# Planning a four-layer graph kernel with repeated forward and backward passes

## The chip, the cores and the metric

The kernel runs on one core of a Trainium2 chip. A core has TensorE (PE: matrix products and transposes, into PSUM), VectorE (DVE), ScalarE (ACT), GpSimd (POOL) and SyncE (SP, which here only issues DMAs). Each engine takes its instructions in the order in which the program lists them and waits for the operands of the one at its head. The metric is the device time of the core in microseconds.

## The reference, cut to what matters

128 graphs of 64 nodes each carry 256 features per node; `adj` holds 0 or 1 for every pair of nodes. Four graph layers follow each other, each on the normalised input and with a residual:

```python
# layer 0: attention with 4 heads, W [256, 256]
h = jnp.maximum(_layernorm(x, axis=-1), 0.0)
x = x + _L0_gnn_ref(h, adj, L0_gnn_W, L0_gnn_a_src, L0_gnn_a_dst)
# layer 1: attention with one head
h = jnp.maximum(_layernorm(x, axis=-1), 0.0)
x = x + _L1_gnn_ref(h, adj, L1_gnn_W, L1_gnn_a)
# layer 2: relational convolution; only relation 1 ("loop") can occur with these edges
h = jnp.maximum(_layernorm(x, axis=-1), 0.0)
x = x + _L2_gnn_ref(h, nodemask, adj, ...)
# layer 3: gated graph convolution, three steps
h = jnp.maximum(_layernorm(x, axis=-1), 0.0)
x = x + _L3_gnn_ref(h, adj, L3_gnn_weight, L3_gnn_w_ih, L3_gnn_w_hh, L3_gnn_b_ih, L3_gnn_b_hh)
```

An attention layer takes `Wh = h @ W`, scores `leaky_relu(e_src[i] + e_dst[j])`, a softmax over the neighbours j of i, and adds `elu(alpha @ Wh)`. The loop relation adds `relu(A^T @ ((h W + b) * sigmoid(h W Wg + bg)))`. A step of layer 3 is a GRU cell:

```python
for i in range(3):
    m = jnp.einsum('bnd,de->bne', h, weight[i])
    aggr = jnp.einsum('bst,bsd->btd', A, m)
    h = _gru_cell(aggr, h, w_ih, w_hh, b_ih, b_hh)   # r, z: sigmoid; n: tanh
```

## The kernel before, in words

**Tiles.** The 8192 rows (graph and node) form 16 groups of four 128-row tiles: 512 rows, eight graphs. All four layers of a group run in SBUF; rows are read once and written once. All is float32. A product streams up to 512 columns through a 128x128 weight; the profile records two passes for each product and one for a transpose.

**Layers 0 to 2** (jobs `(g, p0, layer)`). Each begins with a layer norm and a turned copy `hT`. For groups 0 and 1, which run in halves of two tiles, the turn is made by TensorE transposes (`layernorm_T`); from group 2 on by a 32x32 DVE transpose and 16 DMAs on SP (`layernorm_T_by_dma`, `hT<-hn` in the profile). `attention` needs the source score of every node along the free dimension. From group 2 on it sends it through DRAM: `tp<-fs`, `fT<-tp`, DMA `row<-fT`, two DMAs `t<-row`, all on SP; then DVE makes `t` from it, and `aggregate_graphs` multiplies it with the values in 64x64 quadrants, recorded by `beside` (`mm`, `mn` at L609). `loop_relation` is like it with the edges themselves.

**Layer 3.** Job `("before", g)` normalises and aggregates once more. Job `("recur", g)` runs three GRU steps over transposed states, in two chunks of 128 features (`Chunk`). Products add up in PSUM banks `ry`, `rm`, `rz`, `nh`, `ni`; one bank, `ry`, is filled and emptied in turn by ACT or DVE. The 128-row halves of a state are combined by a seven-product scheme, whose sums of states (`hS`, `aS`) GpSimd makes. DVE ends a step with `d<-z,d` and `hT<-d,t`; `along` aggregates the new state for the next step (`tp`, `tq` at L609, copied to `aT` by ACT). GpSimd makes `d<-hT,t`.

**Weights.** Job `"weights"` transposes the loop relation's weights (`wn`, `gn`) and the GRU's (`hhn`, `ihn`), and multiplies the latter with `weight[i]` (`wrn`). They are loaded by SP in the job "more loads", after the rows of groups 0 and 1.

**What sets the order.** No instruction is issued where it is written. An engine's method (`Engine.__getattr__`; the emitting line is L388, so that nearly every row of the profile says L388) only notes an operation: its engine, its cost in ns from a table, what it reads and writes, its job. `Plan.emit` then places all of them. Each has a due time, worked out from hand-set starts and ends of the jobs (`start, period = 87.96, 83.9`, with offsets for each layer) and from the length of the chain behind the operation; where a job has no end, from its successors. The planner repeatedly takes, among all operations whose predecessors are placed and whose buffers are free, the one that can start first, and of several such the one due first. Engines are modelled with 170.8 ns between them, DMAs as one wire, and DVE and GpSimd as sharing a port. The order in which operations are placed is the program's, and Tile puts the waits between them. Buffers come from pools with a few copies (`Pool.place`, `put`); PSUM's from `Banks`, where, until a bank of layer 3 has been used, the other layers may borrow the first four of those.

Where the model leaves TensorE idle for over 320 ns before 115 us, and layer 3 has not begun, it adds a product of ones that nobody reads for every 220 ns (`nc.spare`, `ni<-warm` at L1322).

Of the kernel before, what the change touches and what calls it, by code (L numbers as in the profile page):

```python
# [45 lines left out]
ENGINES = {"tensor": "PE", "vector": "DVE", "scalar": "Activation", "gpsimd": "Pool", "sync": "SP"}  # L46
# [81 lines left out]
class Base:  # L128


    def __init__(self, pool, shape, dtype, name, tag, bufs):
        self.pool, self.make, self.tag, self.bufs = pool, (shape, dtype, name), tag, bufs
        self.real, self.left, self.end, self.writes, self.reads = None, 0, 0.0, [], []
        self.whole = False


class Pool:
# [5 lines left out]
    def __init__(self, real=None, bufs=1, ordered=()):  # L143
        self.real, self.bufs, self.ordered = real, bufs, ordered
        self.live, self.asked = {}, {}

    def tile(self, shape, dtype, name, tag=None, bufs=None):
        tag = tag or name
        base = Base(self, shape, dtype, name, tag, bufs or self.bufs)
        if tag in self.ordered:  # L150
            self.asked.setdefault(tag, []).append(base)
        return View(base, shape, (), [(0, n) for n in shape], list(range(len(shape))))

    def place(self, base, taken):

        if self.real is None:
            return None
        if base.tag in self.ordered and self.asked[base.tag][0] is not base:
            return None
        live = [b for b in self.live.get(base.tag, ()) if b.left]  # L160
        return base.tag if len(live) + taken.count(base.tag) < base.bufs else None
# [12 lines left out]
    def put(self, base, tag):  # L174
        shape, dtype, name = base.make
        base.real = self.real.tile(shape, dtype, name=name, tag=tag, bufs=base.bufs)
        if base.tag in self.ordered:
            self.asked[base.tag].pop(0)
        live = self.live.setdefault(tag, [])
        if len(live) >= self.room(tag, base):  # L180
            live.remove(min((b for b in live if not b.left), key=lambda b: b.end))
        live.append(base)
# [17 lines left out]
class Job:  # L200
# [3 lines left out]
    def __init__(self, start, end, after):  # L204
        self.start, self.end, self.after, self.left, self.length = start, end, after, 0, 0.0
        self.spread = 1.86


class Plan:
# [21 lines left out]
    def kept(self, pool, shape, dtype, name):  # L231

        view = Pool().tile(shape, dtype, name)
        view.base.real = pool.tile(shape, dtype, name=name)
        return view
# [4 lines left out]
    def note(self, engine, call, cost, writes, reads, after=(), port=0.0, dma=False):  # L240
        op = Op(engine, call, cost, port, dma, self.job, len(self.ops))
        self.ops.append(op)
        self.job.left += 1
# [20 lines left out]
        for b in op.bases:  # L264
            b.left += 1
        return op

    def emit(self):

        self.on = False  # L270
# [11 lines left out]
        for op in self.ops:  # L282
            op.waits = len(op.after)
            for other in op.after:
                other.then.append(op)
# [3 lines left out]
        for op in reversed(self.ops):  # L289
            if op.job.end is None:  # L290
                op.due = 1e9
                for t in op.then:
                    late = 0.0 if t.engine == op.engine else self.LATENCY
                    op.due = min(op.due, t.due - op.job.spread * (op.cost + late))
            else:
                op.due = (op.job.end - (op.job.end - op.job.start) * op.tail / op.job.length) * 1e3
        free = dict.fromkeys([*ENGINES.values(), "-"], 0.0)
        early = {"DVE": 83.0, "Activation": 95.0, "Pool": 43.0}
        ready = {e: [] for e in free}
        wire = 2500.0  # L300
        held = {"DVE": 0.0, "Pool": 0.0}

        def enter(op):
            t = 0.0
            for other, data in op.after.items():
                late = other.end + self.LATENCY
                if other.engine == op.engine and not (other.dma and data):
                    late = other.start if op.engine in ("PE", "SP") or not data else other.end + 35.0
                t = max(t, late)
            op.ready = t  # L310
            ready[op.engine].append(op)

# [3 lines left out]
        left = len(self.ops)  # L316
        while left:
            best = None
            for e, ops in ready.items():
                found = None  # L320
                for op in ops:
                    t = max(free[e], op.ready)
                    if best is not None and t > best[0] or found is not None and t > found[0] and t > free[e]:
                        continue
                    if any(j.left for j in op.job.after):
                        continue
                    places = {}
                    for b in op.needs:
                        if b.real is None:
                            taken = [tag for x, tag in places.items() if x.pool is b.pool]  # L330
                            tag = b.pool.place(b, taken)
                            if tag is None:
                                break
                            places[b] = tag
                            t = max(t, b.pool.released(tag, b, taken.count(tag)))
                    else:
                        key = (t, op.due)
                        if found is None or key < found[:2]:
                            found = (*key, op, places)
                if found is not None and (best is None or found[:2] < best[:2]):  # L340
                    best = found
            assert best is not None, "nothing can be emitted"
            t, _, op, places = best
            e = op.engine
            ready[e].remove(op)
            if e == "PE" and self.spare and t < 115.0 * 1e3:
                for _ in range(int((t - free[e] - 100.0) / 220.0)):
                    self.spare()
            for b, tag in places.items():
                b.pool.put(b, tag)  # L350
            op.call()
            op.start = t
            if op.dma:
                free[e] = t + 665.0
                wire = max(wire, t + 1350.0) + op.cost
                op.end = wire + 400.0
            else:
# [6 lines left out]
                free[e] = t + took - min(early.get(e, 0.0), op.cost / 2)  # L364
# [4 lines left out]
            left -= 1  # L369
            for other in op.then:  # L370
                other.waits -= 1
                if not other.waits:
                    enter(other)
        self.ops = []
        return max(free.values())
# [69 lines left out]
def kernel(  # L445
# [506 lines left out]
    with ExitStack() as s1:  # L952
# [4 lines left out]
        class Banks(Pool):  # L957
# [4 lines left out]
            early = psum = True  # L962
# [8 lines left out]

            def place(self, base, taken):
                if base.tag in self.own:
                    return super().place(base, taken)
                for tag in ("mt", *self.own[: 4 if 115.0 else 5]) if self.early else ("mt",):
# [5 lines left out]
            def put(self, base, tag):  # L981
                base.bufs = self.room(tag, base)
                if base.tag in self.own:
                    self.early = False
                super().put(base, tag)
# [332 lines left out]
        if 115.0:  # L1318
# [3 lines left out]
            nc.spare = lambda: psum.early and nc.nc.tensor.matmul(pause, warm, warm, start=True, stop=True)  # L1322
# [217 lines left out]
```

## Time and profile before

| what | value |
|---|---|
| runs, device time | 1431.6 us median of 3 (1430.19 to 1432.47) |
| profiled execution: span | 1428.7 us |
| median of the runs less that span | 2.9 us |
| PE, share of span | 98% |
| DVE, ACT, POOL | 72%, 57%, 42% |
| DMA | 67.89 MB, mean 48 GB/s |
| warm products (`ni<-warm`) | 242 records, 32.2 us |
| `hT<-hn` DMAs | 896 of 32 KB |

Engine times are busy time; where one engine waits for another and nothing is late for it, the idle time costs nothing. The span is that of one profiled execution, whose durations the rows give; the runs' time includes something before and after it. A float32 product has two records. "Idle before" names what ended the wait of the first instruction behind it.

One group takes about 84 us in the middle of the kernel. While layer 3 of group g runs, TensorE also does layers 0 to 2 of later groups, in the gaps of the recurrence. At the start only groups 0 and 1 and the weights are there; at the end only the last group's recurrence. So three stretches differ: before 115 us, after 1345 us, and between them.

### The profile page before, as it was taken

The numbers are of one execution on the slowest core, as the hardware profiler recorded it, in microseconds if no ns is written. First come the engines' busy times: TensorE is split into PE (matmuls) and PEld (weight loads), VectorE is DVE, ScalarE is ACT, GpSimd is POOL, SyncE is SP. The second block draws the span as 40 slices with busy tenths as digits, with TensorE's granted clock in tenths as the row PEclk, the third lists the DMA queues.
The fourth block names the chain that finished last, engine by engine and source line by source line (L and its number), as shares of the span: only waits on it lengthen the run. The fifth ranks groups of instructions, "written<-read, shape, count | busy, mean of one in ns | idle before, by whom it ended". The sixth has DMA issues, their size and how long they took to land.

```text
span 1428.7 us, 27951 instructions
## 1 busy us (share of the span) xinstructions
PE 1403.0 (98%) x9703; PEld 964.6 (68%) x9703; DVE 1027.9 (72%) x2553; ACT 808.1 (57%) x2045; POOL 600.5 (42%) x744
## 2 busy tenths in 40 slices
PE   9999999999999999999999999999999999999997
PEld 8666666767667666766766676676667666666664
DVE  6658677785958869685886968688686958665544
ACT  3665556565555655655565565556556555554543
POOL 1454344445424444543444354344435434352422
PEclk9999999999999999999999999999999999999998
DMA  8010222222223122222312222231212122111000
GB/s 219 22 20 20 42 60 37 59 44 41 61 49 71 32 63 42 45 60 49 72 31 63 42 46 60 48 72 30 59 28 44 45 45 54 26 22 28 16 15 18
DMA packets 299420, 67.89 MB, mean 48 GB/s; under 512 B 274696, under 2 KB 297480, under 8 KB 299272
## 3 DMA queue, kind: packets, MB, share of 16 engines
q1 hardware_dynamic: 298712, 65.50, 22.0%
q8 instruction: 80, 1.31, 0.4%
q14 instruction: 68, 0.56, 0.1%
q10 hardware_dynamic: 560, 0.52, 0.1%
HBM read 28.06 MB, written 8.53 MB: 26 GB/s over the span
## 4 chain that ended last, share of the span: by engine, by line
PE 88%; DVE 5%; ACT 2%; DMA 2%; SPq 1%; issue 1%; POOL 1%; DVEq 0%; ACTq 0%; POOLq 0%
PE ry L388 22%; PE mm L388 16%; PE rz L388 11%; PE ni L388 10%; PE nh L388 10%; PE rm L388 5%; PE tp L388 4%; PE mm L609 3%; PE tp L609 3%; PE ni L1322 2%; DVE t L388 1%; DMA t<-row 1%; SPq L388 1%; DVE d L388 1%; DVE hT L388 1%
## 5 line engine op out<-in xcount | busy, mean ns | idle before, releaser
L388 POOL TENSOR_TENSOR d<-hT,t 128x256 f32<-128x256 f32 x192 | 143.2, 754 | 485.1 <-ACT t L388 479.8
L388 PE MATMUL ni<-aT,wc 128*128 128x512 f32 x384 | 194.6, 595 | 0.0
L388 PE MATMUL nh<-hT,whh 128*128 128x512 f32 x384 | 193.6, 597 | 0.0
L388 DVE SCALAR_TENSOR_TENSOR t<-r,t 128x256 f32<-128x256 f32 x192 | 110.9, 582 | 66.2 <-ACT r L388 43.4
L388 ACT ACTIVATE z<-z,brz 128x256 f32<-128x256 f32 x192 | 96.8, 504 | 90.4 <-DVE z L388 90.2
L388 ACT COPY z<-ry 128x256 f32<-128x256 f32 x192 | 70.9, 369 | 130.3 <-PE ry L388 86.8
L388 POOL TENSOR_TENSOR hS<-hT 128x256 f32<-128x256 f32 x96 | 79.4, 833 | 121.6 <-PE ry L388 84.5
L388 PE MATMUL ry<-hS,wsum 128*128 128x256 f32 x384 | 117.3, 387 | 2.6 <-ACT z L388 2.6
L388 PE MATMUL rz<-hS,whh 128*128 128x256 f32 x384 | 117.5, 388 | 2.2 <-DVE z L388 2.1
L388 ACT ACTIVATE hn<-xg,var,rstd 128x256 f32<-128x256 f32 x200 | 107.4, 594 | 13.1 <-DVE var L388 12.7
L388 PE MATMUL mm<-wl,hT 128*128 128x512 f32 x248 | 114.7, 597 | 0.1
L388 PE MATMUL ry<-aS,wsum 128*128 128x256 f32 x384 | 114.5, 380 | 0.0
L388 PE MATMUL rz<-aS,wc 128*128 128x256 f32 x384 | 114.4, 380 | 0.0
L388 DVE SCALAR_TENSOR_TENSOR hT<-d,t 128x256 f32<-128x256 f32 x192 | 110.8, 593 | 4.3 <-ACT fd L388 0.5
L388 DVE SCALAR_TENSOR_TENSOR d<-z,d 128x256 f32<-128x256 f32 x192 | 101.1, 537 | 17.2 <-ACT z L388 10.5
L388 ACT ACTIVATE t<-t,bi 128x256 f32<-128x256 f32 x192 | 93.9, 502 | 29.2 <-DVE t L388 28.8
L388 DVE TENSOR_TENSOR t<-t,gd 128x512 f32<-128x512 f32 (+2 forms) x48 | 29.8, 645 | 107.8 <-DMA t<-row 95.3
L388 DVE TENSOR_TENSOR z<-rz,z 128x256 f32<-128x256 f32 x192 | 80.0, 417 | 34.3 <-ACT z L388 17.4
L388 PEld LDWEIGHTS ry<-hS,wsum 128*128 128x128 f32 x384 | 69.4, 190 | 44.5 <-issue 25.3
L388 POOL TENSOR_TENSOR aS<-aT,aS 128x256 f32<-128x256 f32 x96 | 74.0, 772 | 57.8 <-ACT aT L388 57.7
L388 DVE BATCH_NORM_STATS2 st<-xg 128x6 f32<-128x256 f32 x256 | 93.3, 408 | 2.7 <-DMA xg<-in_x_dram 2.7
L388 POOL TENSOR_TENSOR hS<-hT,hS 128x256 f32<-128x256 f32 x96 | 74.7, 778 | 43.9 <-DVE hT L388 43.0
(205 smaller groups left out, 3268.9 us busy)
## 6 DMA issues: line engine op xcount, KB each, us to landing
hT<-hn SPq DMA_DIRECT2D x896, 32.0 KB
xg<-in_x_dram SPq DMA_DIRECT2D x15, 512.0 KB
out_dram<-hnat SPq DMA_DIRECT2D x15, 512.0 KB
t<-row SPq DMA_DIRECT2D x28, 256.0 KB
at<-in_adj_dram SPq DMA_DIRECT2D x64, 32.0 KB
eg<-in_adj_dram SPq DMA_DIRECT2D x64, 32.0 KB
ag<-in_adj_dram SPq DMA_DIRECT2D x16, 128.0 KB
t<-row SPq DMA_DIRECT2D x28, 64.0 KB
```

Of the source, the lines that this page charges most:

```text
L388: return do(*[real(a) for a in args], **{k: real(v) for k, v in kwargs.items()})
L609: nc.nc.tensor.matmul(*[real(x) for x in product], start=True, stop=True)
L1322: nc.spare = lambda: psum.early and nc.nc.tensor.matmul(pause, warm, warm, start=True, stop=True)
```

## The change

The costs, jobs and instructions stay, and so do the hand-set times, for the first pass. The planner is split and repeated. `link` works out the dependencies and the first due times once. `forward` makes a whole order; an engine may now choose, among operations that can start within a leeway of the earliest (100 ns; SP 300), the one due first, and so stand idle until it is ready. `backward` goes through that order's program from its end and gives every operation the latest time at which it could start, counting dependencies, the engine it runs on and the reuse of buffers that this pass had (`replaced`); those are the due times of the next pass. After 40 passes the order with the smallest modelled end is emitted. The pools place buffers in the model and make the tiles when the chosen order is emitted. Warm products are added in that order's idle stretches by the same rule.

```diff
+    PASSES = 40
+    LEEWAY = {"PE": 100.0, "DVE": 100.0, "Activation": 100.0, "Pool": 100.0, "SP": 300.0, "-": 0.0}
+    OVERLAP = {"DVE": 83.0, "Activation": 95.0, "Pool": 43.0}
+    ISSUE = 665.0
+    def link(self):
...
+            op.busy = self.ISSUE if op.dma else op.cost - min(self.OVERLAP.get(op.engine, 0.0), op.cost / 2)
...
+    def forward(self):
+        for b in self.bases:
+            b.left, b.end, b.spot = len(b.ops), 0.0, None
...
             for e, ops in ready.items():
-                found = None
+                leeway, first, found = self.LEEWAY[e], 1e18, []
                 for op in ops:
-                    t = max(free[e], op.ready)
-                    if best is not None and t > best[0] or found is not None and t > found[0] and t > free[e]:
+                    t = op.ready if op.ready > free[e] else free[e]
+                    if t > first + leeway or best is not None and t > best[0] + leeway:
                         continue
...
+                    places, t = spots(op, t)
+                    if places is not None:
+                        first = min(first, t)
+                        found.append((t, op, places))
+                found = [(t, op.due, op, places) for t, op, places in found if t <= first + leeway]
+                if found:
+                    found = min(found, key=lambda f: (f[1], f[0]))
+                    if best is None or found[:2] < best[:2]:
+                        best = found
...
-            if e == "PE" and self.spare and t < 115.0 * 1e3:
-                for _ in range(int((t - free[e] - 100.0) / 220.0)):
-                    self.spare()
...
+            for b, tag in op.places:
+                old = b.pool.put(b, tag)
+                if old is not None:
+                    self.replaced.append((old, op))
...
+    def backward(self, end):
+        before, left = {}, {}
+        for op in self.ops:
+            op.late, op.waits = 1e18, len(op.then)
+            before[op] = []
+        for old, op in self.replaced:
+            for other in old.ops:
+                if other is not op:
+                    before[op].append(other)
+                    other.waits += 1
+        free = dict.fromkeys([*ENGINES.values(), "-"], end)
+        ready = {e: [op for op in self.ops if op.engine == e and not op.waits] for e in free}
+        for op in self.ops:
+            op.took = min(op.end - op.start, 4500.0) if op.dma else op.end - op.start
...
+        for _ in self.ops:
+            best = None
+            for e, ops in ready.items():
+                for op in ops:
+                    key = (min(free[e], op.late + op.busy), op.end)
+                    if best is None or key > best[:2]:
+                        best = (*key, op)
+            t, _, op = best
+            ready[op.engine].remove(op)
+            op.due = free[op.engine] = t - op.busy
+            for other, data in op.after.items():
+                late = op.due - self.LATENCY - other.took
+                if other.engine == op.engine and not (other.dma and data):
+                    late = op.due if op.engine in ("PE", "SP") or not data else op.due - other.took - 35.0
+                limit(other, late)
+            for other in before[op]:
+                limit(other, op.due - self.LATENCY - other.took)
+    def emit(self):
+        self.on = False
+        self.link()
+        best = None
+        for _ in range(self.PASSES):
+            end, order = self.forward()
+            if best is None or end < best[0]:
+                best = end, [(op, op.start, op.idle, op.places) for op in order]
+            self.backward(end)
+        self.ends = best[0]
+        for op, start, idle, places in best[1]:
+            if op.engine == "PE" and self.spare and start < 115.0 * 1e3:
+                for _ in range(int((idle - 100.0) / 220.0)):
+                    self.spare()
+            for b, tag in places:
+                b.pool.make(b, tag)
+            op.call()
...
+            def make(self, base, tag):
+                if base.tag in self.own:
+                    self.spare = False
+                super().make(base, tag)
```

## The prediction

> **What bounds the kernel now.** I read the page's busy times and chain first, then busy time by stage, then the rows of TensorE on both sides of each of its gaps, then the waits of the other engines.
>
> ```profile
> span 1428.7 us, 27951 instructions
> ...
> PE 1403.0 (98%) x9703; PEld 964.6 (68%) x9703; DVE 1027.9 (72%) x2553; ACT 808.1 (57%) x2045; POOL 600.5 (42%) x744
> ...
> PE 88%; DVE 5%; ACT 2%; DMA 2%; SPq 1%; issue 1%; POOL 1%; DVEq 0%; ACTq 0%; POOLq 0%
> ```
>
> TensorE is busy 98% of the span and is 88% of the chain; the next engine has a quarter of its time free. An order changes no product, so it can gain only what TensorE spends on something other than products. Busy time by stage (columns: window, its length, busy us and count of PE, PEld, DVE, ACT, POOL, granted clock, DMA share, GB/s) says where that is:
>
> ```profile
> 0.00:115.00 115.00, 113.26 (x808) 85.96 (x809) 70.05 (x224) 64.45 (x184) 42.51 (x65) 1.00 0.33 86
> 115.00:300.00 185.00, 180.07 (x1304) 120.96 (x1304) 142.03 (x352) 106.64 (x272) 81.92 (x97) 1.00 0.21 44
> 300.00:1130.00 830.00, 827.70 (x5758) 567.69 (x5757) 636.87 (x1552) 484.65 (x1224) 359.02 (x437) 1.00 0.25 50
> 1130.00:1345.00 215.00, 209.41 (x1439) 140.17 (x1438) 140.56 (x342) 116.03 (x285) 93.27 (x116) 1.00 0.16 32
> 1345.00:1429.00 84.00, 72.57 (x400) 49.79 (x400) 38.36 (x87) 36.36 (x84) 23.83 (x33) 0.95 0.05 14
> ```
>
> In the middle 830 us TensorE idles 2.3 us. For a finer measure I took, for each pair of neighbouring product shapes, the usual start-to-start step of the trace, and counted what any step takes beyond it. Such stalls are 2.7 us before 115, 6.6 to 300, 4.2 to 1130, 7.4 to 1345 and 7.7 after: 28.6 us. The last product starts at 1422.6; 6 us of store follow. In the first stage "busy" is partly filler, as the chain shows (start, length, engine, line):
>
> ```profile
> 26.52 8.68 PE ni L1322 x76
> ```
>
> These are 38 warm products in a row, 8.68/38 = 0.228 us each; the kernel has 121 (242 records).
>
> **The change part by part.** *The filler and the start.* Once the changed program is planned, each engine has the same instructions as before, but 95 warm products in place of 121: 26 x 0.228 = 5.9 us of TensorE. Most comes from that gap at 26.5: the new order puts 24 transposes of the gated layer's weights and the first products on them there. So they must have been loaded. On SP's queue their two loads (and four smaller ones) move ahead of group 1's rows and of the edge loads; 3.97 MB must then have arrived. The windows of DMA traffic, the last column in GB/s, give the pace:
>
> ```profile
> 12.00:16.00 4.00, 4.00 (x35) 3.82 (x34) 3.09 (x7) 1.34 (x4) 0.00 (x0) 1.00 1.04 316
> 16.00:20.00 4.00, 4.00 (x22) 3.12 (x21) 0.00 (x0) 2.99 (x15) 1.24 (x2) 1.00 1.10 329
> ```
>
> Up to 16 us (123, 231, 193, 316 GB/s in 4 us each) 3.45 MB; the other 0.52 MB at 329 takes 1.6 us, so 17.6 us, against a use at about 27. Group 1's rows come by some 20 us. The weight work thus ends about 25 us earlier, and the first recurrence begins at 79.7 us of product steps, where it was 85.8. Of this, one stall is given back: between group 0's loop products and its last layer norm's transposes the covering products shrink from 16.1 to 6.6 us, and that chain (product, DVE add, statistics, four ACT normalisations) took 7.5 us, from 72.0 to 79.5; so +0.9. Startup: -5.9 + 0.9 = **-5.0**.
>
> [...] The trace has its first warm products 0.43 us apart until 4.6 us and 0.22 afterwards[...]. By the row no clock is lost, as over 5 us of real products stand where fillers stood. [...] I take the row.
>
> *Short covers.* Most small stalls of before have one shape: TensorE's next product needs a result that another engine makes from a product just issued (columns: start, us, engine, line, operation; in brackets the idle time and what ended it):
>
> ```profile
> 1293.17 0.70 PE L388 MATMUL rz<-hS,whh 128*128 128x256 f32 x2 [0.52 <-DVE z L388]
> ...
> 1398.60 0.70 PE L388 MATMUL ry<-aT,wc 128*128 128x256 f32 x2 [0.89 <-ACT aT L388]
> ...
> 1421.58 0.69 PE L388 MATMUL tp<-ident,hT 128*128 128x128 f32 x2 [2.59 <-DVE hT L388]
> ```
>
> I counted how many us of other products stand between producer and consumer in both orders. For the rz bank (needs 1.11 us start to start) before has three with 0.43 to 0.54, which stalled 1.93 in all; after has none below 1.51: -1.9. The ry bank (needs 0.84) goes from three short ones to one: -1.25. Products on aT (need 0.95) from four at 0.45 (3.85 us of stalls) to three at 0.89, 0.45, 0.02, together 2.0: -1.8. Transposes of the state, but for the last: two to none, about -1.0. Sum **-6.0**. The last wait (2.59 above) has nothing left to cover it in either order: 0.
>
> *Tables through DRAM.* From group 2 on both attentions send a row through DRAM; DVE waits for the result:
>
> ```profile
> DVE t L388 <- DMA t<-row: 95.3, 24, 7.5
> ```
>
> and what stands ahead of it on SP is transposing DMAs at 0.65 us each:
>
> ```profile
> 415.08 0.44 SPq L388 DMA_DIRECT2D row<-fT  x1
> 415.63 1.25 SPq L388 DMA_DIRECT2D hT<-hn  x2
> 416.96 1.20 SPq L388 DMA_DIRECT2D t<-row  x2
> ```
>
> Moving products and DMAs moves this cover. For layer 0's table products cover 11.4 us now and 12.3 to 14.0 after; one stall goes, -0.5. For layer 1's they cover 9.0 in most groups now; after, by group from 3 to 15: 7.8, 8.1, 10.7, 9.1, 13.3, 8.7, 10.7, 9.1, 10.6, 8.1, 8.1, 9.0, 8.2. Where before waited, the trip took 8.6 us; it went unnoticed at 9.1. With 8.6 needed, after is short by 2.7 us (0.8 now): +1.9; with 9.1, by 5.7: +4.9. The measured 8.6 decides. What waits behind the late t on DVE is the recurrence's r and t rows; they then reach TensorE late. Sum **+1.4**.
>
> *Longer trips.* From layer 0's last product to layer 1's first on the transposed rows, products cover 32.6 us in most groups now (33.2 real); after 27.5 (group 2), 31.2 to 31.8 (3, 6, 7, 10, 14) and 32.7 to 35.4 elsewhere. No steady group of before waits there, so 33.2 is enough but may not be needed. Bounds: 0, and, were 32.5 needed (group 2's real trip), 5.0 + 5.2 us; from layer 1 to 2 likewise 0 to 1.8 (group 7). I take 0, for those groups are the nearest row and their waits end on shorter loops.
>
> *DVE and GpSimd.* [...] (busy, mean ns):
>
> ```profile
> L388 DVE SCALAR_TENSOR_TENSOR hT<-d,t 128x256 f32<-128x256 f32 x192 | 110.8, 593 | 4.3 <-ACT fd L388 0.5
> ...
> L388 DVE TENSOR_TENSOR z<-rz,z 128x256 f32<-128x256 f32 x192 | 80.0, 417 | 34.3 <-ACT z L388 17.4
> ```
>
> The first has two SBUF inputs and a median of 418; 117 of the 576 of its kind are stretched, 89 us in all; the second reads PSUM and never is. [...] Doubling the stretched would take DVE from 72% to 78%: by the row 0, since TensorE stays the bound[...]. I take 0.
>
> *The tail.* The last group's recurrence runs alone for 43 us of products rather than 57, because group 14's ends later; the last product still falls 5.9 us earlier, which is the startup's gain arriving, not another. The store after it stays.
>
> Sum on the profiled 1428.7: -5.0 - 6.0 + 1.4 = -9.6, **1419.1**. The median of the runs, 1431.6, is 2.9 above the span: **1422.0**.
>
> **The rivals.** *A, the sum*: 1422, own range 1415 (longer stalls between 115 and 300 shrink too) to 1427 (half of the short covers come back elsewhere).
> *B, better*: stalls left in A's count (28.6 - 6.0 - 3.6 for the last states - 2.7 for the start = 16) mostly follow long chains, and latest-start ranks serve those. Two thirds gone: -9 more, 1413. For: 14 us of them lie in 115-300 and 1130-1345, where hand-set due times fit worst. Against: in the new order these chains' covers are as often shorter as longer.
> *C, no net change*: the filler's time does not travel; recurrence 0 starts earlier but steady groups are paced by their chain, and the short covers reappear. Then only the tail's 2 us remain: about 1430. For: in the new order recurrence 0 ends 1.9 us later in product steps than before. Against: the middle runs TensorE at its pace, so any earlier start should arrive.
> *D, slower*: the trips through DRAM bite at full price: 5.2 + 5.0 + 1.8 + 4.9 = 16.9 us. With -5.0 - 6.0 - 0.5 that is +5.4: 1434.1 profiled, 1437. It decides from 11.5 of the 16.9, or 0.8 us per group from 2 to 15. For: 27.5 us is 1.6 below any cover of before. Against: the planner charges these DMAs too.
>
> **How the numbers follow.** A 0.50, B 0.20, C 0.14, D 0.16. The likeliest gives 1422.0. A tenth lies below 1410 (the lower half of B) and a tenth above 1433 (most of D). A change of 0.2% (2.9 us) is about what a measurement of this kernel can tell from none. Faster: A, B and a quarter of C, 0.74; the same: the rest of C and D's edge, 0.11; slower 0.15.
>
> **What would show it.** Right: 190 warm records rather than 242; TensorE real at 26-35 us; recurrence 0's first ry product near 86 us instead of 91.1; waits of PE on ACT aT and DVE z nearly gone; the 300-1130 stage still some 99.7% busy. Wrong: PE waits of a microsecond or more that end at t, fd or hT of layers 1 and 2 once per group (D); a gap before the first recurrence (C); half clock at 26 us; or TensorE idle by 10 us less in the two ramps (B).

## The result and the profile after

The changed kernel takes **1408.3 us** (median of 4 runs, 1407.0 to 1408.8) against 1431.05 for the kernel before (median of 4): a ratio of **0.984, 95% interval 0.9826 to 0.9854**, so 22.8 us less. The forecast was 1422.0 with 1410 to 1433 as range: the direction was right, but the forecast gain, 9.6 us, is less than half of the measured one, and the time lies 1.7 us below the range. The profiled execution has a span of 1406.1 us:

```profile
span 1406.1 us, 27921 instructions
...
PE 1390.5 (99%) x9651; PEld 962.1 (68%) x9651; DVE 1026.9 (73%) x2553; ACT 811.0 (58%) x2045; POOL 609.7 (43%) x744
...
PE 91%; DVE 3%; SPq 2%; ACT 1%; POOL 1%; DMA 1%; issue 0%; DVEq 0%; POOLq 0%
```

TensorE's records fell by 52: the 26 warm products, two records each. Busy time by stage (window, length, busy us and count of PE, PEld, DVE, ACT, POOL, clock, DMA share, GB/s; the last two windows are moved with the end):

```profile
0.00:115.00 115.00, 113.45 (x808) 85.34 (x809) 73.62 (x229) 70.06 (x199) 46.04 (x71) 1.00 0.31 81
115.00:300.00 185.00, 182.69 (x1311) 123.17 (x1310) 147.59 (x372) 107.56 (x266) 82.92 (x98) 1.00 0.22 47
300.00:1130.00 830.00, 827.66 (x5792) 568.77 (x5791) 635.96 (x1550) 485.50 (x1228) 371.19 (x437) 1.00 0.25 50
1130.00:1325.00 195.00, 195.00 (x1341) 133.88 (x1340) 131.14 (x319) 110.88 (x270) 84.71 (x105) 1.00 0.18 35
1325.00:1406.00 81.00, 71.73 (x404) 50.96 (x402) 38.57 (x87) 37.02 (x84) 24.82 (x35) 0.96 0.05 15
```

The fourth row is the find: TensorE idled 5.6 of 215 us there before and idles not at all now. In the second row the idle time went from 4.9 to 2.3 us. The middle is as it was: 2.3 us idle before and after.

To see where the 22.7 us between the two last products (at 1422.7 and 1400.0) come from, I used one table of usual steps, taken from both traces together, and split each stretch into products at their usual step, stalls over 0.12 us, and the rest, a creep of delays too small to be followed one by one:

| stretch, by first products of recurrences | before | after | products | stalls | creep |
|---|---|---|---|---|---|
| start to recurrence 0 | 90.1 | 85.5 | -6.3 | +1.9 | -0.1 |
| 0 to 3 | 261.6 | 260.9 | +4.1 | -4.2 | -0.6 |
| 3 to 12 | 751.9 | 749.9 | -0.5 | -0.3 | -1.2 |
| 12 to the last product | 318.1 | 302.7 | -3.5 | -10.6 | -1.3 |
| sum | 1421.7 | 1399.0 | -6.1 | -13.2 | -3.3 |

(The stretches start at 1.1 us. The +4.1 and -3.5 of products are work that moved from the end to an earlier place, not work saved.)

### The profile page after: what moved, and what is told of

It is laid out like the page before. It is cut to its first block, busy times and chain, and to the rows that moved or that the text cites. A ratio compares the mean times of both kernels' runs of the same rounds, so it can differ in the third digit from the quotient of the medians.

```text
span 1406.1 us, 27921 instructions
## 1 busy us (share of the span) xinstructions
PE 1390.5 (99%) x9651; PEld 962.1 (68%) x9651; DVE 1026.9 (73%) x2553; ACT 811.0 (58%) x2045; POOL 609.7 (43%) x744
## 4 chain that ended last, share of the span: by engine, by line
PE 91%; DVE 3%; SPq 2%; ACT 1%; POOL 1%; DMA 1%; issue 0%; DVEq 0%; POOLq 0%
PE ry L485 23%; PE mm L485 15%; PE rz L485 12%; PE ni L485 11%; PE nh L485 11%; PE rm L485 6%; PE tp L485 4%; PE mm L706 3%; PE tp L706 3%; SPq L485 2%; PE ni L1427 1%; DVE d L485 1%; DMA t<-row 1%; PE tq L706 1%; ACT hn L485 0%
## 5 line engine op out<-in xcount | busy, mean ns | idle before, releaser
L485 POOL TENSOR_TENSOR d<-hT,t 128x256 f32<-128x256 f32 x192 | 150.8, 794 | 453.3 <-ACT t L485 448.3
L485 PE MATMUL nh<-hT,whh 128*128 128x512 f32 x384 | 196.9, 597 | 0.0
L485 POOL TENSOR_TENSOR hS<-hT 128x256 f32<-128x256 f32 x96 | 77.9, 812 | 143.8 <-PE ry L485 95.4
L485 DVE SCALAR_TENSOR_TENSOR d<-z,d 128x256 f32<-128x256 f32 x192 | 119.3, 644 | 22.2 <-POOL d L485 10.6
L485 DVE SCALAR_TENSOR_TENSOR t<-r,t 128x256 f32<-128x256 f32 x192 | 92.0, 480 | 55.9 <-ACT r L485 46.9
L485 DVE SCALAR_TENSOR_TENSOR hT<-d,t 128x256 f32<-128x256 f32 x192 | 102.9, 558 | 2.5
L485 PEld LDWEIGHTS rz<-hS,whh 128*128 128x128 f32 x384 | 69.1, 190 | 38.7 <-issue 25.3
L485 POOL TENSOR_TENSOR rstd<-var,mhalf 128x4 f32<-128x4 f32 (+1 forms) x70 | 69.9, 999 | 56.3 <-DVE var L485 54.0
```

The costliest lines, as they stand in the source:

```text
L485: return do(*[real(a) for a in args], **{k: real(v) for k, v in kwargs.items()})
```

## The experiments

Every run is compared with runs of the kernel before beside it on the same chip; their median was 1430.55 us for the first four experiments, 1429.98 for the next four and 1429.60 for the last four. So a difference of about 1 us between experiments of different fours means nothing. The first four take the two halves of the change apart, the next four look at the start and at GpSimd, the last four at holding and at a better version.

**Holding without backward ranks**

```diff
-    PASSES = 40
+    PASSES = 1
```

> One pass: the hand-set due times of before, with the leeway of the change. Theory 'ranks' (the due times from backward passes bring the gain): nothing of the 22.8 us comes, and holding for an operation whose hand-set rank is no better costs time: 1428 to 1445 us. Theory 'holding' (an engine that holds for a more urgent operation brings it): at least half of the gain, 1420 us or less. Fillers stand at 130, so the first recurrence should start no earlier than in before (91 us) under both.

Measured: 1450.8 us, ratio 1.0129 (1.0109 to 1.015), on the side of "ranks", but 6 us beyond the most that it had named. The first recurrence starts at 93.0 us. Its stalls are spread over the whole program, as the windows show (same columns as above):

```profile
300.00:1130.00 830.00, 820.86 (x5678) 560.99 (x5677) 622.54 (x1531) 476.02 (x1213) 364.72 (x438) 1.00 0.24 48
1130.00:1365.00 235.00, 227.44 (x1559) 151.91 (x1559) 156.85 (x373) 124.30 (x302) 98.01 (x118) 0.99 0.18 36
```

TensorE idles 9.1 us in the middle, four times what it did before. Holding by hand-set due times makes the kernel slower by 20 us. This fits the reading that an engine which waits for an operation gains only if that operation is truly the more urgent one.

**Backward ranks without holding**

```diff
-    LEEWAY = {"PE": 100.0, "DVE": 100.0, "Activation": 100.0, "Pool": 100.0, "SP": 300.0, "-": 0.0}
+    LEEWAY = {"PE": 0.0, "DVE": 0.0, "Activation": 0.0, "Pool": 0.0, "SP": 0.0, "-": 0.0}
```

> Forty passes, leeway 0 on every engine: an engine takes what can start first and ranks decide only ties. 'Ranks': most of the gain stays, 1408 to 1416 us. 'Holding': the gain goes, 1425 to 1432 us. If both parts are needed the time lies between, about 1418 us.

Measured: 1420.3 us, ratio 0.992 (0.9903 to 0.9936). That is a smaller gain than "ranks" expected and a larger one than "holding" did, nearest to the third number, 1418 if both are needed: ranks alone bring 10.3 of the 22.8 us, and holding, which alone costs 20, brings the other 12 on top of them. (Part of the 12 is the clock, as told below the table of marks.) The two halves of the change are worth nothing like the sum of their single effects.

**TensorE keeps its hand-set due times, the other engines take the ranks**

```diff
             self.backward(end)
+            for op in self.ops:
+                if op.engine == "PE":
+                    op.due = op.hand
```

(`op.hand` is the first due time.)

> Forty passes, but TensorE's operations keep their hand-set due times; the other engines and SP take the backward ranks. Theory 'TensorE's order' (the ranks gain because TensorE issues long chains first): about the time of the one-pass order or before, 1425 us or more. Theory 'the feeders' order' (DVE, ACT, GpSimd and SP serve TensorE sooner): 1415 us or less.

Measured: 1452.5 us, ratio 1.0154 (1.0136 to 1.0173). "The feeders' order" falls; "TensorE's order" had 1425 or more and did not say that the mixture would be 22 us slower than the kernel before. The first recurrence begins at 83.4 us, earlier than in the changed kernel (86.6), and at recurrence 3 it is already later than before (363.6 against 352.7). Here an early start was worth nothing by itself.

**TensorE takes the ranks, the others keep their hand-set due times**

```diff
             self.backward(end)
+            for op in self.ops:
+                if op.engine != "PE":
+                    op.due = op.hand
```

> The other half: only TensorE's operations take the backward ranks, the others keep the hand-set due times. 'TensorE's order': 1408 to 1416 us. 'The feeders' order': 1425 us or more. If each half alone gives part, the gain needs ranks that agree across engines. Fillers stand at 125, so the start should gain nothing.

Measured: 1421.5 us, ratio 0.9932 (0.9916 to 0.9949), between the two theories' numbers. It tells where TensorE's order works. The start is as before (recurrence 0 at 91.2 us), and the last two windows are those of the full change:

```profile
1130.00:1335.00 205.00, 204.92 (x1429) 139.19 (x1430) 138.00 (x340) 115.89 (x284) 93.81 (x113) 1.00 0.17 32
1335.00:1420.00 85.00, 74.89 (x418) 53.78 (x416) 40.51 (x90) 38.26 (x87) 25.18 (x35) 0.96 0.07 17
```

From recurrence 12 on, stalls are 4.8 us, against 15.1 before and 4.4 in the changed kernel. So the gain at the end comes with TensorE's own ranks. What is missing is the start, which belongs to the loads and the feeders, and the stretch up to recurrence 3 (stalls 8.6 us against 3.0). In both mixtures hand-set and backward due times meet in one plan, so they show which engine's ranks matter for a stretch, not the exact worth of each.

**The early weight loads alone, in the planner of before**

```diff
+        moved = {"gn", "wn", "wrn0", "hhn", "ihn"}
+        for op in self.ops:
+            if op.job is self.jobs["more loads"] and op.bases[0].make[2] in moved:
+                moved.remove(op.bases[0].make[2])
+                op.due -= 4e4
```

> The planner of before in one greedy pass; only the loads of five weight tiles (wn, gn, ihn, hhn, wrn0) are given due times 40 us earlier, so that they stand ahead of group 1's rows on SP. Theory of the prediction (weights at work in the filler gap of 26 us bring about 5 us, which travel to the end): first recurrence near 86 us and 1424 to 1427 us. Rival (the gain of the start is lost before the end, since steady groups are paced by their chains): first recurrence near 86 us and 1429 to 1432 us.

Measured: 1435.6 us, ratio 1.0042 (1.0027 to 1.0056), so slower, which neither theory had. Recurrence 0 starts at 86.7 us, as both expected and as in the changed kernel. Then it goes wrong (TensorE rows; in brackets the idle time and what ended it):

```profile
182.00 0.86 PE L393 MATMUL tp<-ident,hT 128*128 128x128 f32 x4 [1.66 <-ACT o L393]
...
200.73 0.48 PE L393 MATMUL ry<-hT,whh 128*128 128x256 f32 x1 [1.12 <-ACT r L393]
...
277.81 0.45 PE L393 MATMUL ry<-hT,whh 128*128 128x256 f32 x1 [1.32 <-DMA hT<-hn]
```

Stalls between recurrences 0 and 3 are 15.5 us where the kernel before had 7.2. The greedy order had moved everywhere, and at recurrence 3 the kernel is 6.5 us behind the one before, though it began 4.4 ahead. The prediction's first step, that the start's microseconds travel to the end, holds only if what follows is ordered to suit.

**Fewer warm products ahead of the first rows**

```diff
-                for _ in range(int((idle - 100.0) / 220.0)):
+                gap = min(idle, 3600.0) if start < 12.0 * 1e3 else min(idle, 1640.0) if start < 16.5 * 1e3 else idle
+                for _ in range(int((gap - 100.0) / 220.0)):
```

> The order of after; the first two blocks of warm products are cut from 38 and 13 to 15 and 7, as the first normalised rows are there at 8.1 us and their transposes start only at 12.4. Theory 'fillers stand in the way': the first transposes start near 8.5 us, the first recurrence 3 to 5 us earlier, 1403 to 1406 us. Theory 'the clock needs them'[...]: products of 8 to 12 us run at half pace and the start gains less than 1 us, 1407 to 1409 us. Third: loads hold the start, no change either.

Measured: 1403.4 us, ratio 0.9809 (0.9792 to 0.9825), 4.9 us below the changed kernel (4.4 by the two ratios), as "fillers stand in the way" had it. The order of real work is the same instruction by instruction. In the changed kernel ACT has the first normalised rows at 8.1 us, and TensorE takes them at 12.4:

```profile
7.00 1.09 ACT L485 ACTIVATE hn<-xg,var,rstd 128x256 f32<-128x256 f32 x2 [0.87 <-DVE var L485]
```

```profile
7.79 4.74 PE L1427 MATMUL ni<-warm 128*128 128x128 f32 x41
...
12.37 0.60 PE L485 MATMUL tp<-ident,hn 128*128 128x128 f32 x4
```

Between them are warm products already queued. With the two blocks cut to 15 and 7 warm products:

```profile
7.38 0.33 PE L486 MATMUL tp<-ident,hn 128*128 128x128 f32 x1 [1.02 <-ACT hn L486]
...
11.35 1.95 PE L486 MATMUL mm<-w0e,hT 128*128 128x264 f32 x8
```

Now TensorE waits for ACT, and recurrence 0 starts at 81.8 us (86.6). With one order, the earlier start does arrive: 3.3 us earlier at the last product of the profiled executions, 4.9 in the medians. (The profiled one is the slowest of the four, and about 1 us of its start was lost to the clock at 141 us, see below.)

**No warm products at all**

```diff
-        if 115.0:
+        if 0:
             warm = const.tile([P, P], F32, name="warm")
```

> The order of after without any warm product. 'Fillers stand in the way': as with the cut ones or 1 us better at the start, 1402 to 1406 us. 'The clock needs them': real products up to 20 us and after each long gap run at half pace; about 10 us of real work before 27 us doubled in part, so 1408 to 1414 us.

Measured: 1406.2 us, ratio 0.983 (0.9813 to 0.9846): not the loss that "the clock needs them" put down, but 2.8 us behind the cut version. Both theories are half right. The same eight records (four products) as in the lines above, and the next eight:

```profile
11.52 3.73 PE L485 MATMUL mm<-w0e,hT 128*128 128x264 f32 x8
...
15.04 2.69 PE L485 MATMUL mm<-w0e,hT0e 128*128 128x264 f32 x8
```

The first eight take 3.73 us instead of 1.95: half pace, up to 16.7 us. Later the granted clock falls twice, for 3.4 us each from 37.0 and from 81.4 us; the last column but two has 0.50 at the first of the two:

```profile
37.10:40.40 3.30, 3.30 (x7) 1.39 (x6) 0.25 (x2) 2.09 (x6) 0.00 (x0) 0.50 0.75 191
```

Removing the fillers lets work begin at 7.2 us, and the half pace eats it up; recurrence 0 starts at 86.7. Full pace came at 16.7 us, some 5 us after the first of these sixteen records (11.5 us).

**GpSimd's residual add in four parts**

```diff
-        engine.tensor_tensor(src, src, em, ALU.add)
+            for p in range(src.shape[1]):
+                nc.nc.gpsimd.tensor_tensor(real(src[:, p]), real(src[:, p]), real(em[:, p]), ALU.add)
```

(noted as one operation of the same cost, so that the order stays.)

> The order of after; GpSimd's residual add of a group (xg<-xg,hn, 128x1024, 2.35 us) is issued as four adds of 128x256 in the same place. Theory 'lock' (at 454.8 and 789.2 us two DVE instructions d<-z,d take 3.4 us behind that add and TensorE stalls about 2 us each time): those two stalls shrink to under 0.5 us and the time falls by 3 to 4 us, 1404 to 1406 us. Rival (the stall is GpSimd being late with d<-hT,t, or DVE does not get in between the parts): no change, 1407 to 1409 us.

The reason for this run is two places of the changed kernel where DVE is held up. Rows of GpSimd and of DVE:

```profile
454.80 2.35 POOL L485 TENSOR_TENSOR xg<-xg,hn 128x1024 f32<-128x1024 f32 x1
```

```profile
454.83 3.46 DVE L485 SCALAR_TENSOR_TENSOR d<-z,d 128x256 f32<-128x256 f32 x2 [0.65 <-POOL d L485]
```

Measured: 1406.7 us, ratio 0.9833 (0.9817 to 0.985), 1.6 us below the changed kernel, with overlapping intervals; it lies just outside both theories' numbers and decides for neither. The same place now:

```profile
454.54 1.83 DVE L485 SCALAR_TENSOR_TENSOR d<-z,d 128x256 f32<-128x256 f32 x2 [0.64 <-POOL d L485]
456.30 1.81 DVE L485 SCALAR_TENSOR_TENSOR hT<-d,t 128x256 f32<-128x256 f32 x2
```

The long stretch is gone (the longest `d<-z,d` fell from 2.59 to 0.97 us), but each of the four DVE instructions is now stretched behind one part, GpSimd's add takes 3.32 us in all instead of 2.35, and DVE is through at 458.1 instead of 459.0 (0.3 us of this it was early before the add). TensorE's stalls in the 20 us after the two adds were not 2 us each but 1.4 and 1.0, and became 1.1 and 0.6. So splitting shares the stretch out more than it removes it. That DVE is held up beside the add is shown (3.46 us for two `d<-z,d` that take 0.76 at 1069.6 us); the price on the path is small. Of the 1.6 us, 1.1 is what the kernel before itself differed by between the two sets of runs.

**Holding by all engines but TensorE, and by TensorE alone**

```diff
+    LEEWAY = {"PE": 0.0, "DVE": 100.0, "Activation": 100.0, "Pool": 100.0, "SP": 300.0, "-": 0.0}   # the first
+    LEEWAY = {"PE": 100.0, "DVE": 0.0, "Activation": 0.0, "Pool": 0.0, "SP": 0.0, "-": 0.0}   # the second
```

> Forty passes; TensorE has no leeway, the other engines keep 100 ns and SP 300. Ranks alone gave 1420, ranks with all leeways 1408. Theory 'TensorE holds' (the last 12 us come from TensorE waiting up to 100 ns for a more urgent product): 1417 to 1421 us. Theory 'the feeders hold' (they come from DVE, ACT, GpSimd and SP not starting a long unimportant operation just before an urgent one): 1407 to 1411 us.

> Forty passes; only TensorE has its leeway of 100 ns. 'TensorE holds': 1407 to 1411 us. 'The feeders hold': 1417 to 1421 us. If both are needed, each alone lies near 1415.

Measured: 1412.5 us, ratio 0.9884 (0.9867 to 0.99), and 1412.4 us, ratio 0.9888 (0.9872 to 0.9905). Neither theory alone, near the 1415 of the third number: with ranks, each half of the holding is worth 8 us by the medians (from 1420.3; 5 by the ratios), and both together 12.

**Longer holding, fewer fillers, the add in parts**

```diff
-    LEEWAY = {"PE": 100.0, "DVE": 100.0, "Activation": 100.0, "Pool": 100.0, "SP": 300.0, "-": 0.0}
+    LEEWAY = {"PE": 100.0, "DVE": 300.0, "Activation": 300.0, "Pool": 300.0, "SP": 600.0, "-": 0.0}
```

with the two edits above (filler blocks cut, the add in four parts).

> The change with DVE, ACT and GpSimd allowed to hold 300 ns and SP 600, the first two filler blocks cut to 15 and 7, and GpSimd's residual add in four parts. The cut was worth about 5 us and the parts about 1.5. If longer holding helps as the first 100 ns did: 1395 to 1399 us; if it does nothing: 1401 to 1403 us; if holding longer costs feeders' time that TensorE then waits for: above 1405 us.

Measured: **1397.0 us**, ratio 0.9779 (0.9763 to 0.9795): 11.3 us below the changed kernel, inside the 1395 to 1399 of longer holding that helps. Its windows:

```profile
115.00:300.00 185.00, 183.16 (x1279) 123.99 (x1278) 147.62 (x377) 109.57 (x270) 86.69 (x113) 1.00 0.22 46
300.00:1130.00 830.00, 829.48 (x5807) 571.82 (x5809) 626.95 (x1562) 492.70 (x1230) 382.91 (x498) 1.00 0.25 50
```

In the middle TensorE idles 0.5 us in 830. Recurrence 0 starts at 77.9 us, 3.9 before the version with cut fillers alone. The cut and the parts account for about 6.5 us of the 11.3 by their own runs; the other 5 are put to the order from longer holding by subtraction, since that was not run alone. The run below, taken beside this one, has the cut without parts or longer holding and is 5.9 us slower, which agrees; by the ratios the 11.3 are 8.7. Another run of the planner with other leeways would give another order, so a few microseconds of this may be the luck of one plan.

**Fewer fillers later, too**

```diff
+                gap = min(idle, 3600.0) if start < 12.0 * 1e3 else min(idle, 1640.0) if start < 16.5 * 1e3 else idle * 0.7
```

> The order of after with the first two filler blocks cut and every later one cut to 0.7 of its gap (45 warm products instead of 66). Theory 'fillers stand in the way' in the later gaps too: 1 to 3 us better than with 66, 1400 to 1402 us. Theory 'the chain of group 0 holds the start': 1402 to 1404 us, with idle time on TensorE in place of the fillers. If the clock falls in the longer gaps, slower than 1404.

Measured: 1402.9 us, ratio 0.982 (0.9803 to 0.9836), the same as with 66 warm products (1403.4) and in the range of the second theory. After 17 us the chain of group 0 holds the start, not the fillers.

Stalls over 0.12 us after recurrence 0 and the marks of each profiled execution, in us:

| kernel | recurrence 0 starts | recurrence 3 | recurrence 12 | last product | stalls after recurrence 0 |
|---|---|---|---|---|---|
| before | 91.1 | 352.7 | 1104.6 | 1422.7 | 26.5 |
| hold only | 93.0 | 362.9 | 1120.8 | 1444.2 | 45.8 |
| TensorE hand-set | 83.4 | 363.6 | 1122.0 | 1444.0 | 52.3 |
| early loads | 86.7 | 359.2 | 1108.7 | 1426.5 | 32.1 |
| ranks only | 87.0 | 350.9 | 1101.7 | 1413.2 | 23.6 |
| TensorE ranks | 91.2 | 359.0 | 1110.2 | 1413.2 | 17.1 |
| changed kernel | 86.6 | 347.4 | 1097.3 | 1400.0 | 11.4 |
| fillers cut | 81.8 | 344.5 | 1094.1 | 1396.7 | 12.5 |
| long hold | 77.9 | 339.4 | 1085.5 | 1388.5 | 7.0 |

Some of these stalls are the clock's. In eight of the fourteen traces the granted clock falls to 0.50 for 3.41 us, once for 6.83, well before the last products: five times in "hold only", twice in "early loads" and without warm products, once in "ranks only" (the 6.83, from 149 us on), "TensorE hand-set", "fillers cut" and each half of the holding. The kernel before, the changed kernel and "long hold" have none. In the table this is, by an estimate from the stalls in those stretches, about 6 us of "hold only", 4 of "ranks only", 2 of "early loads" and 1 each of "TensorE hand-set" and "fillers cut". The last has the order of the changed kernel; the windows on both sides of the fall:

```profile
137.80:141.10 3.30, 1.53 (x37) 1.04 (x36) 3.30 (x10) 2.77 (x7) 1.87 (x3) 1.00 0.03 7
141.20:144.50 3.30, 3.30 (x9) 1.87 (x7) 3.30 (x10) 1.40 (x4) 3.20 (x5) 0.50 0.07 11
```

TensorE was not idle for 3.4 us there; it was busy for 1.53 of 3.30. So waits that together fill half of such a stretch can cost up to 1.7 us more (an estimate, half of 3.41) when the next products run at half pace, and by the same estimate an order that keeps TensorE fed would save that too.

## Why the prediction was wrong

**The start was right in size.** The sum had -5.0; recurrence 0 starts 4.5 us earlier. Fillers went as counted, 26 of them. The first two blocks now, 38 and 13 warm products (two records each):

```profile
1.06 11.47 PE ni L1427 x76
...
12.97 2.90 PE ni L1427 x26
```

The give-back, 1.9 us of stalls where 0.9 was named, was another than the one named: half of it is five more warm products at half pace in this first block (until 6.9 us, where before it was 4.6), half small waits of 0.2 to 0.5 us at six places between 29 and 84 us. And the 8.7 us gap at 26 us did not vanish altogether: 15 of its 38 warm products are left between 26.8 and 34 us, and the block at 80 us grew from 6 to 12. That 5 us at the start reach the end was taken for granted; the early loads show that they need not.

**The step that failed is "short covers", with rival A's assumption that the other stalls stay.** It counted four kinds of short dependency, -6.0, and left some 16 us of stalls as they were, because their covers were as often shorter as longer in the new order. Measured, stalls after recurrence 0 fell by 15.1 us, from 26.5 to 11.4, and creep by another 3.1. Of the stalls, 10.6 went from recurrence 12 on. TensorE's waits of over 0.15 us from 86 us on, by what ended them (us in all, times, longest), before:

```profile
PE tp L388 <- DVE hT L388: 3.9, 5, 2.6
PE ry L388 <- ACT z L388: 3.5, 5, 1.2
PE ry L388 <- ACT aT L388: 2.7, 3, 0.9
PE rz L388 <- DVE z L388: 2.1, 6, 0.5
PE rm L388 <- DVE r L388: 1.7, 4, 0.7
```

and in the changed kernel:

```profile
PE tp L485 <- DVE hT L485: 3.1, 3, 2.5
PE rm L485 <- DVE hT L485: 1.8, 1, 1.8
...
PE ry L485 <- ACT aT L485: 0.7, 1, 0.7
PE rm L485 <- DVE r L485: 0.6, 2, 0.3
```

The first four rows are the four kinds. Three of them came as forecast: transposes of the state 0.8 less (forecast 1.0), products on aT 2.0 (1.8), the rz bank 2.1 (1.9). The ry bank was mis-sized: all 3.5 us of this list went, where the sum had 1.25. With the rows not shown, these waits fell from 17.9 to 7.8 us, the four kinds by 8.4 of the 10.1; with the small ones down to 0.12 us, sorted in the same way, the four kinds lost about 10 us where 6.0 was forecast. The rm bank (1.1 less) was put at nothing, and a wait of 1.3 us on the tables of layer 0, at 202 us, at 0.5. One wait on the state, of 1.8 us at 145, is new.

The longest ry wait of before shows what the count could not see (TensorE's two rows, then ACT's, DVE's and GpSimd's):

```profile
1270.75 0.59 PE L388 MATMUL ry<-aS,wsum 128*128 128x256 f32 x2
...
1274.28 0.70 PE L388 MATMUL ry<-hS,wsum 128*128 128x256 f32 x2 [1.21 <-ACT z L388]
...
1273.85 0.37 ACT L388 COPY z<-ry 128x256 f32<-128x256 f32 x1 [2.41 <-DVE d L388]
...
1271.19 2.55 DVE L388 SCALAR_TENSOR_TENSOR d<-z,d 128x256 f32<-128x256 f32 x1 [0.29 <-POOL d L388]
...
1271.11 2.35 POOL L388 TENSOR_TENSOR xg<-xg,hn 128x1024 f32<-128x1024 f32 x1
```

Other products kept TensorE busy until 1272.9, 2.1 us after the start of the last product into the bank, and the bank needs 0.84: the cover is long. But ACT could not empty the bank, since its copy waited for DVE's `d<-z,d`, and that took 2.55 us beside GpSimd's add. At 1213 us the same copy was late because DVE had a `hn<-hn,o` of 1.22 us ahead of `d<-z,d`. The count of covers says how much work stands in between; it doesn't say how soon DVE, ACT and GpSimd get to the chain. The runs show that these orders matter together: with holding, ranks for TensorE alone brought 9.0 us and ranks for all 22.8; without holding, ranks for all brought 10.3.

The rows at the end that answer to the four kinds:

```profile
1376.44 0.70 PE L485 MATMUL ry<-aT,wc 128*128 128x256 f32 x2 [0.73 <-ACT aT L485]
...
1398.90 0.44 PE L485 MATMUL tp<-ident,hT 128*128 128x128 f32 x2 [2.54 <-DVE hT L485]
```

The rz bank's stalls at the end are gone as forecast, one wait on aT is left there, and the last wait on the state stays (2.54 for 2.59), also as forecast. Rival B had the other stalls go, and its sign came: TensorE idles 8.2 us less in the second and fourth window. It put -9 on this, 1413 (two thirds of its 16 us would be -10.7); with the DRAM step below and the creep it would have come near the measured time. That is in part luck, for some of it is waits of the kinds already counted, and the creep was in nobody's sum. What shortened the creep is not shown.

**Tables through DRAM, +1.4, was wrong.** The cover for layer 1 shrank as computed (8.1 us in groups 12 and 13), but only one stall of 0.5 us, at group 3, came of it. The trip needs less than the 8.6 us taken from the two places where before waited: in the changed kernel it took 8.2 at group 12, and nothing waited. SP's and DVE's rows for group 13:

```profile
1072.02 0.45 SPq L485 DMA_DIRECT2D row<-fT  x1
1072.51 1.74 SPq L485 DMA_DIRECT2D hT<-hn  x2
1074.35 1.20 SPq L485 DMA_DIRECT2D t<-row  x2
```

```profile
1071.32 0.28 DVE L485 COPY fT<-tp 4x128 f32<-4x128 f32 x1 [0.31 <-PE tp L485]
1077.72 0.42 DVE L485 TENSOR_TENSOR t<-t,gd 128x256 f32<-128x256 f32 x1 [6.12 <-DMA t<-row]
```

DVE copied fT by 1071.6 and SP issued its row 0.4 us later; at the place that the prediction showed, 1.5 us went by (413.6 to 415.1). The wait itself also got smaller in all:

```profile
DVE t L485 <- DMA t<-row: 55.1, 15, 6.5
```

It was 95.3 us in 24 waits. **The longer trips** that were taken at 0 did cost nothing that shows, and with them rival D falls: group 2's cover of 27.5 us was real at 29.9, below the 32.5 that was its upper bound.

**DVE and GpSimd, taken at 0.** In all, little changed: the time beyond the median in stretched `d<-z,d`, `hT<-d,t` and `t<-r,t` went from 89 to 83 us. `d<-z,d` is stretched more now (first row: before) and `hT<-d,t` less (110.8 us before):

```profile
L388 DVE SCALAR_TENSOR_TENSOR d<-z,d 128x256 f32<-128x256 f32 x192 | 101.1, 537 | 17.2 <-ACT z L388 10.5
...
L485 DVE SCALAR_TENSOR_TENSOR d<-z,d 128x256 f32<-128x256 f32 x192 | 119.3, 644 | 22.2 <-POOL d L485 10.6
...
L485 DVE SCALAR_TENSOR_TENSOR hT<-d,t 128x256 f32<-128x256 f32 x192 | 102.9, 558 | 2.5
```

The 4.0 us of stalls left between recurrences 3 and 12 all lie in the recurrences of groups 4 and 8, and 2.3 of them follow within 20 us the two adds told of with the split add. The stretching bears on the path after all, in both kernels, where a 128x1024 add of GpSimd meets the state of a recurrence (`d<-z,d` took 2.55 us at 1271 us before, above; two of them took 3.46 and 3.42 us at 454.8 and 789.2 in the changed kernel); what the split took away of the two stalls was 0.7 us.

**The clock.** The row was rightly taken for this change, since nothing idled at 26 us. But its granted clock of 1.00 proves less than it was taken to. Without fillers, products run at half pace until 16.7 us while the profile's window has 1.00 there:

```profile
12.00:17.00 5.00, 5.00 (x14) 3.90 (x13) 0.69 (x1) 1.36 (x8) 1.04 (x1) 1.00 1.05 333
```

The falls later in a run do stand in the row, at 0.50, for 3.41 us (once 6.83). No idle stretch of that length came before them: in the 3.4 us ahead of each of the fourteen TensorE was still busy for 0.32 to 0.52 of the time.

What is left open: how the gain divides between ranks and holding in general, since each plan is one outcome of a search and the two interact; what taking the best of 40 orders is worth by itself, since no run has fewer passes but the one with a single pass; and whether the gain at the end would be as large without the work that the new order moved ahead (3.5 us of products left the last stretch).

## What to carry to other kernels

Judge a new order by every chain that ends in a wait of the bounding engine, with the order of all engines on it; a count of the work between two products on that engine alone put 6 us here on waits that fell by about 10, and nothing on the others, which with the creep brought some 8 more. Treat rules for choosing and the ranks that they choose by as one thing: holding for the urgent operation cost 20 us with hand-set ranks and brought 12 with ranks from a backward pass. And look at what is queued ahead of the first real work: warm products that are there for the clock cost 5 us when there are more of them than the wait is long, and 3 us when there are none.

## What the runs showed of the hardware

- TensorE's pace at the start is not in the granted clock that a window prints: without warm products, 264-column products took 0.88 us a step instead of 0.44 up to 16.7 us with a clock of 1.00 in the row. There the step between equal products is the better sign. The switch, from 0.21 to 0.11 us between records of warm products, came at 4.6 us before and at 6.9 us in the changed kernel, though both begin them at 1.06 us.
- In the middle of a run the granted clock fell to 0.50 fourteen times in eight traces, for 3.41 us each and once for 6.83. It took no idle stretch of that length: without warm products, the 3.3 us ahead of the fall at 37.0 us had TensorE busy for 1.64 us, and its longest single wait there was 0.9 us.
- Two DVE instructions on 128x256 with two SBUF inputs took 3.46 us behind one GpSimd add of 128x1024, the longest single one 2.59 us where its median is 0.42. In four parts, the add took 3.32 us instead of 2.35, and no `d<-z,d` or `hT<-d,t` more than 1.0 us.
